# Two attentions over an image: group statistics by transfers, and Wk folded into the query projection

## The chip, the cores and the metric

The kernel runs on one core of one Trainium2 chip. The metric is device time in microseconds of one execution, taken as the median of several runs. A core has a matrix engine (TensorE, PE in the profile, with its weight loads shown as PEld), a vector engine (VectorE, DVE), an activation engine (ScalarE, ACT), GpSimd (POOL), an engine that here only starts transfers (SyncE, SP), and 16 DMA engines.

## The reference, cut to what matters

Two attention layers follow each other over x of shape (8, 64, 64, 64), that is 8 images of 64 channels and 4096 positions, all float32. Layer 0 has keys and queries of 8 channels and no scaling. Layer 1 normalises by groups of 8 channels first, has 64 channels of keys and queries, and a projection of its output.

```python
# layer 0 (n = 4096 positions, C8 = 8)
f = einsum('oc,bcn->bon', Wf, xf) + bf
g = einsum('oc,bcn->bon', Wg, xf) + bg
hh = einsum('oc,bcn->bon', Wh, xf) + bh
beta = softmax(einsum('bci,bcj->bij', f, g), axis=2)
x = x + einsum('bcj,bij->bci', hh, beta)

# layer 1
xg = x.reshape(b, 8, 8, h, w)              # 8 groups of 8 channels
mu = mean(xg, axis=(2, 3, 4)); var = mean((xg - mu) ** 2, axis=(2, 3, 4))
xn = (xg - mu) * rsqrt(var + 1e-5) * gamma + beta
q, k, v = split(einsum('oc,bchw->bohw', w_qkv, xn) + b_qkv, 3, axis=1)
attn = softmax(einsum('bqc,bkc->bqk', q, k) * 64 ** -0.5)
out = einsum('bqk,bkc->bqc', attn, v)
x = einsum('oc,bchw->bohw', w_proj, out) + b_proj + x
```

## The kernel before

Batch b is one image. The 4096 positions of an image lie in two halves of 2048: partitions 0 to 63 hold the channels of the first half and 64 to 127 those of the second. A half is four chunks of 512 columns. Each layer of each image is a stage of four chunks by 16 steps. In a step of layer 1, TensorE makes scores (8 products of 64x64 weights by 512 columns), ScalarE takes their exponential into a tile e, and TensorE weighs the values with the e of the step before; VectorE adds all e of a chunk into esum for the denominators. The stages come in the order layer 0 of image 0, layer 0 of image 1, layer 1 of image 0, layer 0 of image 2, layer 1 of image 1, and so on, and end with layer 1 of image 7. The scores of layer 0 come in groups of up to seven banks, fewer where another piece of work takes a pair of banks in that step.

PSUM has eight banks. Two accumulate, and six are three pairs which scores and everything else take in turn:

```python
    pairs = [banks[:, 2 * k + 1 : 2 * k + 3, :] for k in range(3)]
    ...
    def pair():
        nonlocal turn
        if lent is not None:
            return pairs[lent]
        turn += 1
        return pairs[turn % 3]
```

gavg is a constant that averages over the eight channels of a group and both halves, as a matrix product:

```python
    gavg = const.tile([P, 2, GROUPS, GS], F32, name="gavg")
    nc.gpsimd.memset(gavg, 0.5 / GS)
        ...  # affine_select keeps only the channels of the own group
```

What layer 1 of one image needs is prepared during an earlier stage, in units of (step, work, whether it takes a pair of banks). For image 0 that stage is layer 0 of image 1; for image b from 1 on it is layer 1 of image b - 1:

```python
        def before(self):
            ...
            def channels():
                vector.bn_aggr(mv, self.st())

            def means():

                ps = pair()
                matmul(ps[:, 0, 0:1], gavg, mv[:, 0:1], start=True, stop=True)
                nc.scalar.copy(mu, ps[:, 0, 0:1])
                d = small.tile([P, 1], F32, tag="d", name=f"d_{n}")
                vector.tensor_sub(d, mv[:, 0:1], mu)
                vector.scalar_tensor_tensor(v, d, d, mv[:, 1:2], op0=ALU.mult, op1=ALU.add)

            def deviations():
                ps = pair()
                matmul(ps[:, 0, 0:1], gavg, v, start=True, stop=True)
                ve = small.tile([P, 1], F32, tag="ve", name=f"ve_{n}")
                nc.scalar.copy(ve, ps[:, 0, 0:1])
                vector.tensor_scalar_add(ve, ve, EPS)
            ...  # four Newton steps for 1 / sqrt(ve), then times gamma, into self.a

            def normal(c):
                xns[c] = work.tile([P, CW], F32, tag="xn", bufs=1, name=f"xn_{n}_{c}")
                vector.tensor_scalar(
                    xns[c], x_tiles[self.b][:, ts(c, CW)], mu, self.a,
                    op0=ALU.subtract, op1=ALU.mult,
                )

            def begin():
                self.parts = self.own(F32)
                self.project(0, xns[0])

            at = [18, 22, 26] if self.b == 0 else [16, 20, 24]
            units = [(at[0], channels, False), (at[1], means, True), (at[2], deviations, True)]
            for c in range(NC):
                s = 31 + 8 * c if self.b == 0 else 30 + 8 * c
                units += [
                    (s - 4, lambda c=c: normal(c), False),
                    (s, begin if c == 0 else lambda c=c: self.project(c, xns[c]), True),
                    (s + 2, lambda c=c: self.values(xns[c], k1["wvp"], c), True),
                ]
            return units

        def project(self, c, xn):


            ps = pair()
            for i in range(2):
                for h in range(2):
                    matmul(
                        ps[ts(h ^ i, C), h, :], k1["wqk"][ts(h, C), i, :], xn[ts(h, C), :],
                        start=True, stop=True,
                    )
            cols = ts(c, CW)
            for h in range(2):
                nc.scalar.activation(
                    self.parts[:, h, cols], ps[:, h, :], AF.Identity,
                    bias=k1["qkb"][:, h : h + 1],
                )
                nc.sync.dma_start(
                    self.parts[ts(h, C), 2, cols], self.parts[ts(1 - h, C), h, cols]
                )

        def scores(self, ps, t, p, c):
            for m in range(2):
                for h in range(2):
                    matmul(
                        ps[ts(m, C), h, :],
                        self.parts[ts(h, C), 2 if p == h else 1 - h, ds(t * P + m * C, C)],
                        self.parts[ts(h, C), h, ts(c, CW)], start=True, stop=True,
                    )
```

`self.own` takes one of two buffers of a tile kq of (128, 3, 2048): part h holds q of half h in the partitions of that half and k of half h in the opposite ones, and part 2 takes k over into the partitions of its own half by a transfer, so that products of every half with every half find key and query in the same partitions. The weights Wv and Wproj are already multiplied into wvp before the start. The constants of layer 1 are made in three turns (`transposed`, `product`, `biases`) during the second chunk of layer 0 of image 0, each of which takes a pair of banks.

Of the kernel before, what the change touches and what calls it, by code (L numbers as in the profile page):

```python
# [9 lines left out]
F32 = mybir.dt.float32  # L10
# [58 lines left out]
def fast_path(  # L69
# [52 lines left out]
    made_last = {}  # L122
    tight = False
# [25 lines left out]
    def matmul(*args, **kwargs):  # L149
        in_order(nc.tensor.matmul(*args, **kwargs))  # L150

# [79 lines left out]
    gavg = const.tile([P, 2, GROUPS, GS], F32, name="gavg")  # L231
    nc.gpsimd.memset(gavg, 0.5 / GS)
    for h in range(2):
        for half in range(2):
            rows = gavg[ts(half, C), h, :, :]
            nc.gpsimd.affine_select(
                out=rows, in_=rows, compare_op=ALU.is_ge, fill=0.0,
                base=0, pattern=[[-GS, GROUPS], [0, GS]], channel_multiplier=1,
            )
            nc.gpsimd.affine_select(  # L240
                out=rows, in_=rows, compare_op=ALU.is_ge, fill=0.0,
                base=GS - 1, pattern=[[GS, GROUPS], [0, GS]], channel_multiplier=-1,
            )
    gavg = gavg.rearrange("p h g s -> p (h g s)")


    QP = 2 * CW // P
    stash = const.tile([P, (2 * B * NC - 1) * QP], F32, name="stash")
    recips = [dram.tile([P, QP], F32, name=f"recips_{i}") for i in range(2 * B * NC)]
# [3 lines left out]
    def layer1_constants():  # L253


        wqk = const.tile([P, 2, C], F32, name="wqk")
        for h in range(2):
            nc.gpsimd.dma_start(
                wqk[ts(h, C), :, :], WqkvT[:, 0 : 2 * C].rearrange("m (i c) -> m i c", i=2)
            )  # L260
        wp = twice("wp", WpT)
        wv = const.tile([C, C], F32, name="wv")
        nc.gpsimd.dma_start(wv, WqkvT[:, 2 * C : 3 * C])

        qkb = const.tile([P, 2], F32, name="qkb")
        for h in range(2):
            for i in range(2):
                nc.gpsimd.dma_start(
                    qkb[ts(h, C), i : i + 1], column(bqkv[ds(C if i != h else 0, C)])
                )  # L270
# [4 lines left out]
        wvt = const.tile([C, 2, C], F32, name="wvt")  # L275
        wvp = const.tile([P, C], F32, name="wvp")
        more = const.tile([P, 3], F32, name="more")
        k1.update(wqk=wqk, qkb=qkb, gam=gam, pb=pb, wvp=wvp)

        def transposed():  # L280
            t0 = pair()
            in_order(nc.tensor.transpose(t0[:C, 0, 0:C], wv, ident[0:C, 0:C]))
            for h in range(2):
                nc.scalar.copy(wvt[:, h, :], t0[:C, 0, 0:C])

        def product():
            t1 = pair()
            matmul(
                t1[:, 0, 0:C], wvt.rearrange("m h c -> m (h c)"), wp[0:C, :],
                start=True, stop=True,  # L290
            )
            nc.scalar.copy(wvp, t1[:, 0, 0:C])

        def biases():
            t2 = pair()
            for h in range(2):
                rows = ts(h, C)
                for i in range(2):
                    matmul(
                        t2[rows, h, i : i + 1], wqk[rows, i ^ h, :], bet[rows, :],  # L300
                        start=True, stop=True,
                    )
                matmul(t2[rows, h, 2:3], wvp[rows, :], bet[rows, :], start=True, stop=False)
                matmul(t2[rows, h, 2:3], wp[rows, :], vb[rows, :], start=False, stop=True)
            for h in range(2):
                nc.scalar.copy(more[ts(h, C), :], t2[ts(h, C), h, 0:3])
# [1012 lines left out]
```

## Time and profile before

| | |
|---|---|
| time, median of 3 runs | 3051.95 us (3050.56 to 3053.05) |
| span of the profiled execution | 3050.3 us |
| TensorE busy | 3023.2 us, 25857 matmul records |
| VectorE busy | 2596.0 us |
| ScalarE busy | 2036.3 us |
| L150 PE MATMUL banks<-xn_l,wqk (the projection of q and k) | 256 records, 35.5 us |
| L669 ACT ACTIVATE kq_l<-banks,qkb (its copies out of PSUM) | 64, 40.6 us |
| PE MATMUL banks<-mv_l,gavg and banks<-v_l,gavg (the statistics) | 16 records each, 3.0 and 3.1 us |
| DMA queues | 62.89 MB, mean 21 GB/s |

A group is named by source line, engine, operation, and what it writes and reads (output <- inputs, partitions x elements). All matrix products have line 150 and nearly all VectorE work line 140, since helpers record them, so groups are told apart by their tiles. A float32 product shows as two records, one per pass. Busy times overlap between engines; a share of busy time does not say which engine sets the end, for which there is the chain of work that ended last, followed back from the last instruction. The ends of matmuls are modelled, so their starts are the surer reading.

### The profile page before, as it was taken

How to read it: one execution, taken by the hardware profiler on the slowest of the kernel's cores; microseconds unless marked ns; L12 is line 12 of the kernel's file. 1: busy time of each engine (PE TensorE's matmuls, PEld its weight loads, DVE VectorE, ACT ScalarE, POOL GpSimd, SP SyncE). 2: the span in 40 equal slices, each digit the busy share in tenths (PEclk: the TensorE clock that was granted, in tenths of full speed). 3: DMA queues.
4: the chain of work that ended last, by engine and by line, in shares of the span. 5: the costliest groups of instructions: out<-in, count | busy, mean ns of one | idle time of the engine just before them, and what ended most of it. 6: DMA issues, size and time to landing. Idle time of an engine off the chain costs nothing.

```text
span 3050.3 us, 58859 instructions
## 1 busy us (share of the span) xinstructions
PE 3023.2 (99%) x25857; PEld 1287.4 (42%) x25857; DVE 2596.0 (85%) x1668; ACT 2036.3 (67%) x1972; POOL 16.7 (1%) x45
## 2 busy tenths in 40 slices
PE   8999999999999999999999999999999999999998
PEld 3333335433354333533345333453334533345555
DVE  6999987899778998789987899779997799877776
ACT  6878655786557865578655785558855588555554
POOL 2000000000000000000000000000000000000000
PEclk9999999999999999999999999999999999999999
DMA  3000010100101001010010100100001000000000
GB/s 79 22 8 11 19 40 16 32 1 15 40 19 29 1 15 40 22 25 1 16 40 23 25 1 15 43 22 22 1 22 40 19 8 1 16 22 16 9 15 13
DMA packets 69816, 62.89 MB, mean 21 GB/s; under 512 B 43104, under 2 KB 43152, under 8 KB 69552
## 3 DMA queue, kind: packets, MB, share of 16 engines
q1 hardware_dynamic: 68560, 58.90, 8.0%
q8 instruction: 204, 3.34, 0.5%
q14 instruction: 60, 0.49, 0.1%
q0 software_dynamic: 672, 0.12, 0.0%
q10 hardware_dynamic: 320, 0.04, 0.0%
HBM read 25.06 MB, written 8.65 MB: 11 GB/s over the span
## 4 chain that ended last, share of the span: by engine, by line
PE 95%; DVE 3%; issue 1%; ACT 1%; DMA 0%; SPq 0%; DVEq 0%; ACTq 0%
PE banks L150 95%; DVE esum_l L140 3%; ACT e_l L917 1%; DMA x<-in_x_dram 0%; ACT full_l L542 0%; DVE rt L140 0%; DVE w_l L140 0%; DVE x L140 0%; SPq L179 0%; DVE raw_l L140 0%; DVE st_l L140 0%; DVE raw_end L140 0%; DVE guess_l L140 0%; DVE xn_l L140 0%; DVEq L140 0%
## 5 line engine op out<-in xcount | busy, mean ns | idle before, releaser
L140 DVE TENSOR_TENSOR esum_l<-esum_l,e_l 128x2048 f32<-128x2048 f32 x895 | 2048.7, 2289 | 363.5 <-ACT e_l L876 313.5
L876 ACT ACTIVATE e_l<-banks 128x1024 f32<-128x1024 f32 x1024 | 992.7, 1021 | 782.8 <-PE banks L150 761.0
L150 PE MATMUL banks<-e_l,v_l 64*64 64x512 f32 (+2 forms) x8772 | 1118.2, 588 | 0.0
L917 ACT ACTIVATE e_l<-banks 128x512 f32<-128x512 f32 (+3 forms) x767 | 956.9, 1311 | 194.0 <-PE banks L150 178.1
L150 PE MATMUL banks<-kq_l 64*64 64x512 f32 (+1 forms) x8448 | 1028.3, 586 | 3.4 <-ACT e_l L917 3.2
L150 PE MATMUL banks<-e_l,vt_l 128*64 128x512 f32 (+1 forms) x4060 | 832.1, 550 | 0.0
L150 PEld LDWEIGHTS banks<-e_l,v_l 64*64 64x64 f32 (+1 forms) x8772 | 439.7, 134 | 505.0 <-issue 466.8
L150 PEld LDWEIGHTS banks<-kq_l 64*64 64x64 f32 (+1 forms) x8448 | 422.9, 135 | 503.8 <-issue 468.3
L150 PEld LDWEIGHTS banks<-e_l,vt_l 128*64 128x64 f32 x4060 | 267.1, 137 | 471.3 <-issue 451.2
L150 PE MATMUL banks<-fg_l 32*128 32x512 f32 x1792 | 210.8, 460 | 6.4 <-ACT e_l L917 4.1
L150 PEld LDWEIGHTS banks<-fg_l 32*128 32x128 f32 x1792 | 85.9, 183 | 189.9 <-ACT e_l L917 139.1
L140 DVE TENSOR_TENSOR esum_l<-e_l,e_l 128x2048 f32<-128x2048 f32 x64 | 146.4, 2287 | 7.1 <-ACT e_l L876 7.1
L140 DVE TENSOR_TENSOR esum_l<-esum_l 128x1024 f32<-128x1024 f32 x63 | 76.9, 1221 | 0.9
L140 DVE TRANSPOSE_TENSOR_REDUCE part_l<-esum_l 128x32 f32<-128x1024 f32 x32 | 63.1, 1973 | 0.0
L140 DVE COPY raw_l<-banks 128x512 f32<-128x512 f32 x31 | 21.4, 692 | 30.6 <-PE banks L150 30.6
L140 DVE TENSOR_TENSOR raw_l<-raw_l,r_l 128x512 f32<-128x512 f32 x63 | 43.2, 685 | 0.0
L669 ACT ACTIVATE kq_l<-banks,qkb 128x512 f32<-128x512 f32 x64 | 40.6, 696 | 0.0
L150 PE MATMUL banks<-xn_l,wqk 64*64 64x512 f32 x256 | 35.5, 592 | 0.0
L150 PEld LDWEIGHTS banks<-wh,x 64*64 64x64 f32 x1024 | 25.3, 139 | 13.3 <-issue 12.4
L150 PEld LDWEIGHTS banks<-wvp,xn_l 64*64 64x64 f32 x1024 | 24.0, 134 | 13.0 <-issue 13.0
L577 ACT COPY raw_l<-banks 128x512 f32<-128x512 f32 x32 | 19.1, 596 | 11.6 <-PE banks L150 11.4
L140 DVE SCALAR_TENSOR_TENSOR x<-raw_l,hb,x 128x512 f32<-128x512 f32 x32 | 24.1, 752 | 1.1
(111 smaller groups left out, 404.4 us busy)
## 6 DMA issues: line engine op xcount, KB each, us to landing
r_l<-recips SPq DMA_DIRECT2D x126, 128.0 KB, 2.9
fg_l<-high_l SPq DMA_DIRECT2D x216, 64.0 KB, 2.0
kq_l<-kq_l SPq DMA_DIRECT2D x64, 128.0 KB, 2.3
out_dram<-raw_l SPq DMA_DIRECT2D x62, 128.0 KB, 2.4
x<-in_x_dram SPq DMA_DIRECT2D x30, 256.0 KB, 4.9
kq_l<-high_l SPq DMA_DIRECT2D x32, 64.0 KB, 2.0
part_l<-part_l SPq DMA_DIRECT2D x128, 4.0 KB, 1.8
zt_l<-zs_l SPq DMA_DIRECT2D x124, 1.0 KB, 1.7
```

The source lines that it names most:

```text
L140: it = getattr(nc.vector, name)(*args, **kwargs)
L150: in_order(nc.tensor.matmul(*args, **kwargs))
L577: nc.scalar.copy(raw, acc[0])
L669: nc.scalar.activation(self.parts[:, h, cols], ps[:, h, :], AF.Identity, bias=k1["qkb"][:, h : h + 1],)
L876: nc.scalar.activation(e[:, p], both_ps[p], AF.Exp, scale=at.scale)
L917: nc.scalar.activation(e.rearrange("k p h n -> k (p h) n")[:, first_ : first_ + n_, :], banks[:, bank : bank + n_, :], AF.Exp, scale=at.scale,
```

## The change

Two things change in layer 1.

The first is the statistics. The averages over a group of channels no longer come from products with gavg. VectorE's mean and variance of each channel (mv) are stored to DRAM, and four transfers bring to each partition the 16 pairs of its group, over both halves; VectorE reduces them. This frees TensorE and ScalarE and the pairs of banks of that work.

The second is the keys. Scores are q . k = (Wq x + bq) . (Wk x + bk), and the term with bk is the same for all keys of a query, so the softmax drops it. What is left is (Wk' Wq x + Wk' bq) . x: one matrix, made once, projects the query, and the keys are the normalised x itself. So a chunk needs half as many product columns: four products of 256 columns in place of four of 512. The normalised x now has a place of its own in the tile kq for the whole stage, and its copy with halves swapped is made by the same number of transfers as before, as soon as it is normalised. The constants need one more turn (`bias_kq`).

The new work is issued behind the last addition into esum (`behind`), which fixes its place in VectorE's order. The diff, cut:

```diff
+    def behind(work_):
+        def made():
+            with tc.issue_after(added):
+                work_()
+        return made
...
-    gavg = const.tile([P, 2, GROUPS, GS], F32, name="gavg")
-    nc.gpsimd.memset(gavg, 0.5 / GS)
...
+    moments = [dram.tile([P, 2], F32, name=f"moments_{b}") for b in range(B)]
...
         def transposed():
-            t0 = pair()
-            in_order(nc.tensor.transpose(t0[:C, 0, 0:C], wv, ident[0:C, 0:C]))
+            ps = pair()
+            for i in range(3):
+                in_order(nc.tensor.transpose(ps[:C, 0, ts(i, C)], w3[:, i, :], ident[0:C, 0:C]))
             for h in range(2):
-                nc.scalar.copy(wvt[:, h, :], t0[:C, 0, 0:C])
+                nc.scalar.copy(
+                    wt[:, :, h, :], ps[:C, 0, 0 : 3 * C].rearrange("m (i c) -> m i c", i=3)
+                )
 
         def product():
-            t1 = pair()
-            matmul(
-                t1[:, 0, 0:C], wvt.rearrange("m h c -> m (h c)"), wp[0:C, :],
-                start=True, stop=True,
-            )
-            nc.scalar.copy(wvp, t1[:, 0, 0:C])
+            ps = pair()
+            for i, (left, right) in enumerate(((wt[:, 0], wt[:, 1, 0, :]), (wt[:, 2], wp[0:C, :]))):
+                matmul(
+                    ps[:, i, 0:C], left.rearrange("m h c -> m (h c)"), right,
+                    start=True, stop=True,
+                )
+            nc.scalar.copy(wkq_wvp, ps[:, :, 0:C])
 
         def biases():
-            t2 = pair()
+            ps = pair()
+            matmul(ps[:C, 0, 0:1], w3[:, 0, :], bet[0:C, :], start=True, stop=True)
             for h in range(2):
                 rows = ts(h, C)
-                for i in range(2):
-                    matmul(
-                        t2[rows, h, i : i + 1], wqk[rows, i ^ h, :], bet[rows, :],
-                        start=True, stop=True,
-                    )
-                matmul(t2[rows, h, 2:3], wvp[rows, :], bet[rows, :], start=True, stop=False)
-                matmul(t2[rows, h, 2:3], wp[rows, :], vb[rows, :], start=False, stop=True)
-            for h in range(2):
-                nc.scalar.copy(more[ts(h, C), :], t2[ts(h, C), h, 0:3])
-            nc.vector.tensor_add(qkb, more[:, 0:2], qkb)
-            nc.vector.tensor_add(pb, more[:, 2:3], pb)
-
-        return [transposed, product, biases]
+                matmul(ps[rows, 1, 0:1], wvp[rows, :], bet[rows, :], start=True, stop=False)
+                matmul(ps[rows, 1, 0:1], wp[rows, :], vb[rows, :], start=False, stop=True)
+            nc.scalar.activation(qb, ps[:C, 0, 0:1], AF.Identity, bias=qb)
+            nc.scalar.activation(pb, ps[:, 1, 0:1], AF.Identity, bias=pb)
+
+        def bias_kq():
+            ps = pair()
+            matmul(
+                ps[:, 0, 0:1], wt[:, 1].rearrange("m h c -> m (h c)"), qb, start=True, stop=True
+            )
+            nc.scalar.copy(kqb, ps[:, 0, 0:1])
+
+        return [transposed, product, biases, bias_kq]
 
 
...
+            group = small.tile([P, 2, GS, 2], F32, tag="group", bufs=1, name=f"group_{n}")
+            mean, var = (group[:, :, :, i].rearrange("p s k -> p (s k)") for i in range(2))
+            d = small.tile([P, 2 * GS], F32, tag="d", bufs=1, name=f"d_{n}")
             def channels():
                 vector.bn_aggr(mv, self.st())
+                sent = moments[self.b]
+                nc.sync.dma_start(sent, mv)
+                for s in range(2):
+                    rows = sent[ts(s, C), :].rearrange("(g k) i -> g (k i)", k=GS)
+                    for h in range(2):
+                        nc.sync.dma_start(
+                            group[ts(h, C), s, :, :],
+                            rows.unsqueeze(1).broadcast_to([GROUPS, GS, 2 * GS]),
+                        )
             def means():
-                ps = pair()
-                matmul(ps[:, 0, 0:1], gavg, mv[:, 0:1], start=True, stop=True)
-                nc.scalar.copy(mu, ps[:, 0, 0:1])
-                d = small.tile([P, 1], F32, tag="d", name=f"d_{n}")
-                vector.tensor_sub(d, mv[:, 0:1], mu)
-                vector.scalar_tensor_tensor(v, d, d, mv[:, 1:2], op0=ALU.mult, op1=ALU.add)
+                vector.tensor_reduce(mu, mean, axis=AX.X, op=ALU.add)
+                vector.tensor_scalar(mu, mu, 0.5 / GS, None, op0=ALU.mult)
+                vector.tensor_scalar(d, mean, mu, None, op0=ALU.subtract)
+                vector.tensor_mul(d, d, d)
+                vector.tensor_add(d, d, var)
+                vector.tensor_reduce(ve, d, axis=AX.X, op=ALU.add)
             def deviations():
-                ps = pair()
-                matmul(ps[:, 0, 0:1], gavg, v, start=True, stop=True)
-                ve = small.tile([P, 1], F32, tag="ve", name=f"ve_{n}")
-                nc.scalar.copy(ve, ps[:, 0, 0:1])
-                vector.tensor_scalar_add(ve, ve, EPS)
+                vector.tensor_scalar(ve, ve, 0.5 / GS, EPS, op0=ALU.mult, op1=ALU.add)
                 guess = small.tile([P, 1], I32, tag="guess", name=f"guess_{n}")
                 vector.tensor_single_scalar(
...
                 vector.tensor_mul(self.a, y, k1["gam"])
             def normal(c):
-                xns[c] = work.tile([P, CW], F32, tag="xn", bufs=1, name=f"xn_{n}_{c}")
+                if c == 0:
+                    parts = self.own(F32)
+                    self.q, self.x, self.swapped = (parts[:, i, :] for i in range(3))
+                cols = ts(c, CW)
                 vector.tensor_scalar(
-                    xns[c], x_tiles[self.b][:, ts(c, CW)], mu, self.a,
+                    self.x[:, cols], x_tiles[self.b][:, cols], mu, self.a,
                     op0=ALU.subtract, op1=ALU.mult,
                 )
-
-            def begin():
-                self.parts = self.own(F32)
-                self.project(0, xns[0])
-
-            at = [18, 22, 26] if self.b == 0 else [16, 20, 24]
-            units = [(at[0], channels, False), (at[1], means, True), (at[2], deviations, True)]
+                for h in range(2):
+                    nc.sync.dma_start(self.swapped[ts(h, C), cols], self.x[ts(1 - h, C), cols])
+            at = [18, 23, 26] if self.b == 0 else [16, 22, 24]
+            units = [
+                (at[0], channels, False),
+                (at[1], behind(means), False),
+                (at[2], behind(deviations), False),
+            ]
             for c in range(NC):
                 s = 31 + 8 * c if self.b == 0 else 30 + 8 * c
                 units += [
-                    (s - 4, lambda c=c: normal(c), False),
-                    (s, begin if c == 0 else lambda c=c: self.project(c, xns[c]), True),
-                    (s + 2, lambda c=c: self.values(xns[c], k1["wvp"], c), True),
+                    (s - 4, behind(lambda c=c: normal(c)), False),
+                    (s, lambda c=c: self.project(c), True),
+                    (s + 2, lambda c=c: self.values(self.x[:, ts(c, CW)], k1["wvp"], c), True),
                 ]
             return units
-        def project(self, c, xn):
+        def project(self, c):
             ps = pair()
+            width = CW // 2
+            cols = [ds(c * CW + i * width, width) for i in range(2)]
             for i in range(2):
                 for h in range(2):
                     matmul(
-                        ps[ts(h ^ i, C), h, :], k1["wqk"][ts(h, C), i, :], xn[ts(h, C), :],
-                        start=True, stop=True,
+                        ps[ts(h ^ i, C), i, 0:width], k1["wkq"][ts(h, C), :],
+                        self.x[ts(h, C), cols[i]], start=True, stop=True,
                     )
-            cols = ts(c, CW)
+            nc.scalar.activation(
+                self.q[:, cols[0]], ps[:, 0, 0:width], AF.Identity, bias=k1["kqb"]
+            )
             for h in range(2):
+                other = ts(1 - h, C)
                 nc.scalar.activation(
-                    self.parts[:, h, cols], ps[:, h, :], AF.Identity,
-                    bias=k1["qkb"][:, h : h + 1],
-                )
-                nc.sync.dma_start(
-                    self.parts[ts(h, C), 2, cols], self.parts[ts(1 - h, C), h, cols]
+                    self.q[ts(h, C), cols[1]], ps[other, 1, 0:width], AF.Identity,
+                    bias=k1["kqb"][other, :],
                 )
         def scores(self, ps, t, p, c):
             for m in range(2):
                 for h in range(2):
+                    keys = self.x if p == h else self.swapped
                     matmul(
-                        ps[ts(m, C), h, :],
-                        self.parts[ts(h, C), 2 if p == h else 1 - h, ds(t * P + m * C, C)],
-                        self.parts[ts(h, C), h, ts(c, CW)], start=True, stop=True,
+                        ps[ts(m, C), h, :], keys[ts(h, C), ds(t * P + m * C, C)],
+                        self.q[ts(h, C), ts(c, CW)], start=True, stop=True,
                     )
```

## The prediction

> **What bounds the kernel now.** I read the page first: busy shares, then the chain that ended last.
>
> ```profile
> PE 3023.2 (99%) x25857; PEld 1287.4 (42%) x25857; DVE 2596.0 (85%) x1668; ACT 2036.3 (67%) x1972; POOL 16.7 (1%) x45
> ...
> PE 95%; DVE 3%; issue 1%; ACT 1%; DMA 0%; SPq 0%; DVEq 0%; ACTq 0%
> ```
>
> TensorE (PE) is busy 99% of the 3050.3 us span and carries 95% of the chain. A busy PE need not be a PE at its peak, so I looked at how the chain lies in time (columns: start, length, what).
>
> ```profile
> 264.71 2.30 DVE esum_l L140
> 267.03 1.23 DVE esum_l L140
> 268.72 2.21 DVE esum_l L140
> 272.95 294.58 PE banks L150 x2778
> 570.39 107.73 PE banks L150 x606
> 678.14 265.03 PE banks L150 x2524
> 946.04 107.72 PE banks L150 x604
> 1053.77 265.03 PE banks L150 x2517
> ```
>
> There are two regimes. From about 145 to 273 us, where layer 0 of batches 0 and 1 runs with nothing of layer 1 beside it, the chain is mostly one 2.3 us VectorE addition into esum after another. From 272.95 us on it is PE, repeating with a period of 1053.77 - 678.14 = 375.63 us: one layer-1 stage and one layer-0 stage per batch. Seven of the eight layer-1 stages prepare the next batch's layer 1, and there the change acts. So I read TensorE in time inside the first of them (start, length, what).
>
> ```profile
> 404.96 1.90 PE L150 MATMUL banks<-e_l,v_l 64*64 64x512 f32 x16
> 406.68 1.90 PE L150 MATMUL banks<-kq_l 64*64 64x512 f32 x16
> 408.50 0.38 PE L150 MATMUL banks<-mv_l,gavg 128*128 128x1 f32 x2
> 408.81 1.95 PE L150 MATMUL banks<-e_l,v_l 64*64 64x512 f32 x16
> 410.58 1.90 PE L150 MATMUL banks<-kq_l 64*64 64x512 f32 x16
> ...
> 420.88 1.90 PE L150 MATMUL banks<-kq_l 64*64 64x512 f32 x16
> 422.71 0.38 PE L150 MATMUL banks<-v_l,gavg 128*128 128x1 f32 x2
> 423.02 1.95 PE L150 MATMUL banks<-e_l,v_l 64*64 64x512 f32 x16
> 424.79 1.90 PE L150 MATMUL banks<-kq_l 64*64 64x512 f32 x16
> ...
> 442.81 1.90 PE L150 MATMUL banks<-kq_l 64*64 64x512 f32 x16
> 444.53 1.04 PE L150 MATMUL banks<-xn_l,wqk 64*64 64x512 f32 x8
> 445.39 1.90 PE L150 MATMUL banks<-e_l,v_l 64*64 64x512 f32 x16
> 447.11 1.47 PE L150 MATMUL banks<-kq_l 64*64 64x512 f32 x12
> ```
>
> Read the starts, not the lengths (ends are modelled and overlap). Scores to weighing, or weighing to scores, is always 1.715 us: 16 records, which are 8 products in two passes, four at a time in the four 64x64 quarters, so four rounds of 0.429 us. A whole step is 3.43 us (410.58 to 414.01, and so on). What stands between scores and weighing comes wholly on top: nothing hides it.
>
> **What the Trainium skill says.** "TensorEngine Tiling (Array Packing)", section Key Properties: tiles work independently, and changing the tiling mode drains the engine. The trace agrees: a 128x1 product with gavg moves one column, yet the step around it, 406.68 to 410.58, is 3.90 us instead of 3.43, 0.47 us more, and the weighing after it starts slowly too (1.77 us instead of 1.715). "TensorE: Matmul & The Clock Gate", section Back-to-back issue gap: a product's spacing is N/2.4 ns plus 2.5 for N columns at the full clock, with a floor of about 60 cycles. For 512 columns that is 0.216 us. The trace has 0.429 us per round, twice as much, so here one pass costs two cycles per column; of the page I keep only that the spacing goes with the columns. A round of 256 columns is then estimated at 0.215 us. "ScalarE: Activation LUTs", section What ACT_TABLE_LOAD costs: an ACTIVATE with a bias pointer takes about 280 + 0.833 N ns. For N = 512 that is 706; the page has 696 for kq_l<-banks,qkb. For 256 it gives an estimate of 0.49 us. "DMA: Bandwidth & Descriptors", section Two DMAs through the same engine are not ordered: a transfer that reads what another wrote must wait for the first one's completion. So the statistics take two latencies in a row; for small transfers the page shows 1.4 us (recips) and 1.7 (zt).
>
> **The change part by part.**
>
> *Projection.* Before: four products of 512 columns per chunk, one round in each of two passes. Step 442.81 to 447.11 is 4.30 us, so 0.865 over 3.43. After: four of 256 in the same four quarters, 2 x 0.215 = 0.43. Saved 0.43 per chunk, four chunks per stage: 1.73 us.
>
> *Statistics.* Two products with gavg leave the PE: 3.90 - 3.43 = 0.47, and 424.79 - 420.88 - 3.43 = 0.48, so 0.95 us per stage. In their place: one store of mv, four loads of group, and on VectorE two reductions (about 0.20 each, as zt_l<-part_l) and four small operations (about 0.155) for one of 0.15 and one of 0.22: 1.02 - 0.37 = 0.65 us more per batch. VectorE is busy 179.8 of the 227 us from 345 to 572, so this lies beside the PE. Wait for the loads: store 1.4, four issues of about 0.6 (the part_l transfers need 2.56 us for four), landing 2 or 3, so about 7 us; aggregation at step 16 and use at step 22 are six steps apart, 20.6 us. Hidden. The sixteen fg transfers behind them in the queue start some 5 us later and are not needed until the stage ends, over 100 us on.
>
> *Keys.* The normalised x is written into the kq tile and swapped by the same 64 transfers of 128 KB (2.3 us), only four steps earlier; needed a stage later. Hidden. There are two buffers of kq, and the one taken was last read a whole stage earlier, so taking it four steps sooner waits for nothing.
>
> *ScalarE.* Two evictions of 696 ns become one of 128x256 and two of 64x256, about 0.49 each: 1.47 against 1.39 us. After a projection ScalarE idles 1.20 us before the next exponential, so it fits, and the pair of banks is needed only one step later.
>
> *Once only.* Constants get two more transposes, one more product and a fourth turn that takes a pair of banks in layer 0 of batch 0; there a smaller group of scores costs one more change of tiling, about 0.4 us. Estimated +0.5 us, at about 110 us where the chain is still PE.
>
> *Layer 0 of batch 1* (145 to 337 us) prepares the first layer 1. The PE loses four projections (1.7 us) and two gavg products that each took a pair; VectorE gains 0.65 us, and loses the 0.62 us that it waited for ve_l. VectorE is the chain until 273 us; after it the PE is, but VectorE is at 96%. I count -0.8 us.
>
> Sum: seven stages x (1.73 + 0.95) = 18.8; +0.5 - 0.8; in all -19.1 us: 3051.95 - 19.1 = 3032.9, rounded to 3033.
>
> **Rivals.**
> First, a round of 256 columns isn't half as long, because four weight loads or a fixed cost bound it. Against: the value products (64 columns, 32 records, eight rounds) stretch a step by 450.54 to 454.44 less 3.43 = 0.47 us, 0.059 per round, so the loads keep up far below 0.215. If it were so all the same, only 7 x 0.95 would be left: 3045.
> Second, VectorE or a late transfer becomes the wait. VectorE runs its additions in order, so a late group would hold every following addition, then the e tiles, then ScalarE and PE. For: at 145 to 273 us it is already the chain, and there only five steps of about 2.3 us, 11.5 us, lie between aggregation and use. Against: 7 us suffices. If the first batch misses by a few us: 3036 to 3038; if all batches did (not believed, 13 us of slack): up to 3055.
> Third, ScalarE's three smaller evictions hold back the next exponentials. It would show as PE waits of about 0.1 to 0.3 us in 28 steps, at most 8 us: 3041. Against it the 1.20 us of idle time.
> Fourth, the smaller groups and their rearrangement in layer 0 of the first two batches (28 more products of 256 columns stand in place of 14 of 512) cost 2 or 3 us: 3036.
>
> **Range and chances.** The seven stages are regular to 0.01 us and carry nearly all; what is loose is the stretch before 340 us, give or take 2 us, the repeats, which spread over 2.5 us, and a small part for the rivals, all on the slow side. So 3029 to 3038. 2% is 61 us; the groups of PE that the change shortens or removes are busy for 35.5 us (xn_l by wqk) and 6.1 us (both with gavg) in all, so faster by over 2% is as good as excluded, and slower needs a wait of 10 us per stage, which nothing shows.
>
> **What would show it.** The period 678 to 1053 should fall from 375.63 to 372.95 us. The step with a projection should take 3.86 us, and no step at the statistics over 3.43. The group kq_l by wkq_wvp should hold 256 records of 256 columns. DVE should not idle ahead of the first reduction of group. If the projection step takes 4.3 the first rival holds; if mu_l waits for a transfer, the second; if PE waits for the evictions of kq_l, the third. A layer-0 stage of other than 107.7 us on the chain would mean that something moved that I didn't see.

## The result, and the profile after

| | before | after |
|---|---|---|
| time, median of 4 runs each | 3052.5 us (3050.56 to 3053.83) | 3035.34 us (3034.77 to 3036.53) |
| ratio, after to before | | 0.9945, 95% interval 0.9928 to 0.9962 |
| span of the profiled execution | 3050.3 us | 3033.1 us |

So the changed kernel is 17.2 us shorter (0.55%), where 19.1 us was predicted: 3035.3 against 3033, inside the range of 3029 to 3038, and within 2%.

The busy shares and the shares of the chain that ended last, after:

```profile
PE 3003.4 (99%) x25853; PEld 1320.3 (44%) x25853; DVE 2597.6 (86%) x1698; ACT 2040.7 (67%) x1988; POOL 10.6 (0%) x31
...
PE 93%; DVE 4%; issue 1%; ACT 1%; DMA 0%; SPq 0%; DVEq 0%; ACTq 0%
```

TensorE is still the bound. Its busy time fell by 19.8 us, and its share of the chain by two points. The chain in time, after (start, length, what), shows the period:

```profile
568.77 107.71 PE banks L151 x596
676.49 262.39 PE banks L151 x2515
941.75 107.71 PE banks L151 x595
1049.47 262.37 PE banks L151 x2506
...
2541.77 479.48 PE banks L151 x4454
```

1049.47 - 676.49 = 372.98 us, where 375.63 was the period before. The pieces of 107.71 us (107.73 before) are the first part of a layer-0 stage, not the whole of it: the stage goes on until the first weighing of the next layer 1, at 716.31 us (717.95 before), 39.82 us behind 676.49 (before: 39.81 us behind 678.14). So nothing came out of the layer-0 stage, and all of it out of the layer-1 stage. TensorE in time, in the first layer-1 stage after (start, length, what), shows where:

```profile
411.13 1.90 PE L151 MATMUL banks<-kq_l 64*64 64x512 f32 x16
412.85 1.90 PE L151 MATMUL banks<-e_l,v_l 64*64 64x512 f32 x16
414.56 1.90 PE L151 MATMUL banks<-kq_l 64*64 64x512 f32 x16
...
442.89 1.90 PE L151 MATMUL banks<-kq_l 64*64 64x512 f32 x16
444.61 0.61 PE L151 MATMUL banks<-kq_l,wkq_wvp 64*64 64x256 f32 x8
445.04 1.90 PE L151 MATMUL banks<-e_l,v_l 64*64 64x512 f32 x16
446.75 1.90 PE L151 MATMUL banks<-kq_l 64*64 64x512 f32 x16
```

Where the products with gavg stood, scores now follow each other in 414.56 - 411.13 = 3.43 us. The step with a projection takes 446.75 - 442.89 = 3.86 us, and its weighing starts 0.43 us later than it would without one (445.04 - 444.61). The groups of the changed work (form, count, busy us, mean ns of one, idle before):

```profile
L151 PE MATMUL banks<-kq_l,wkq_wvp 64*64 64x256 f32 x256 | 21.8, 379 | 0.0
L685 ACT ACTIVATE kq_l<-banks,kqb 64x256 f32<-64x256 f32 x64 | 30.1, 470 | 1.2
L680 ACT ACTIVATE kq_l<-banks,kqb 128x256 f32<-128x256 f32 x32 | 15.3, 478 | 0.0
```

The projection is 21.8 us where it was 35.5. Its copies are 45.4 us where they were 40.6, and the idle column of L685 holds 1.2 us that did not exist before.

Divided at the same points, the two chains account for the whole difference (us):

| stretch | before | after | difference | predicted |
|---|---|---|---|---|
| start to the first weighing of layer 1 of image 0 | 342.30 | 343.32 | +1.02 | +0.5 - 0.8 = -0.3 |
| from there to the same product inside layer 0 of image 2 (678.14, 676.49) | 335.84 | 333.17 | -2.67 | -2.68 |
| five periods (to 2556.33, 2541.77) | 1878.19 | 1865.28 | -12.91 | -13.40 |
| the rest, with the seventh such stage | 493.97 | 491.33 | -2.64 | -2.68 |
| sum | 3050.3 | 3033.1 | -17.20 | -19.1 |

Two places miss. In the five periods, one (1422.44 to 1795.80) is 0.39 us longer than its neighbours. And in the first 343 us, which should have gained a little, the change loses. The runs below first split the gain, and then look for that loss.

In that early stretch the starts of two runs differ by up to 1.8 us, so I count from one mark: the start of VectorE's last addition of the first chunk of layer 0 of image 0 (68.44 us before, 67.69 after). From there to the first weighing it is 273.86 us before and 275.63 after: a loss of 1.77 us.

### The profile page after: what moved, and what is told of

It is laid out like the page before. It is cut to its first block, busy times and chain, and to the rows that moved or that the text cites. A ratio compares the mean times of both kernels' runs of the same rounds, so it can differ in the third digit from the quotient of the medians.

```text
span 3033.1 us, 58936 instructions
## 1 busy us (share of the span) xinstructions
PE 3003.4 (99%) x25853; PEld 1320.3 (44%) x25853; DVE 2597.6 (86%) x1698; ACT 2040.7 (67%) x1988; POOL 10.6 (0%) x31
## 4 chain that ended last, share of the span: by engine, by line
PE 93%; DVE 4%; issue 1%; ACT 1%; DMA 0%; SPq 0%; DVEq 0%; ACTq 0%
PE banks L151 93%; DVE esum_l L141 3%; ACT e_l L923 1%; DMA x<-in_x_dram 0%; ACT full_l L539 0%; DVE x L141 0%; DVE st_l L141 0%; DVE raw_l L141 0%; DVE high_l L141 0%; ACT kq_l L685 0%; DVE rt L141 0%; DVE w_l L141 0%; SPq L189 0%; DVE raw_end L141 0%; DVE guess_l L141 0%
## 5 line engine op out<-in xcount | busy, mean ns | idle before, releaser
L151 PE MATMUL banks<-e_l,v_l 64*64 64x512 f32 (+1 forms) x8792 | 1122.3, 586 | 0.0
L923 ACT ACTIVATE e_l<-banks 128x1536 f32<-128x1536 f32 (+3 forms) x766 | 956.8, 1312 | 195.9 <-PE banks L151 180.1
L151 PEld LDWEIGHTS banks<-e_l,v_l 64*64 64x64 f32 (+1 forms) x8792 | 459.3, 133 | 484.8 <-issue 427.7
L151 PEld LDWEIGHTS banks<-kq_l 64*64 64x64 f32 (+1 forms) x8448 | 440.6, 135 | 488.5 <-issue 443.5
L685 ACT ACTIVATE kq_l<-banks,kqb 64x256 f32<-64x256 f32 x64 | 30.1, 470 | 1.2
L151 PEld LDWEIGHTS banks<-wkq_wvp,kq_l 64*64 64x64 f32 x1024 | 24.8, 134 | 12.6 <-issue 11.9
L151 PE MATMUL banks<-wh,x 64*64 64x64 f32 x1024 | 24.2, 223 | 0.3 <-ACT full_l L539 0.3
```

The costliest lines, as they stand in the source:

```text
L685: nc.scalar.activation(self.q[ts(h, C), cols[1]], ps[other, 1, 0:width], AF.Identity, bias=k1["kqb"][other, :],)
L923: nc.scalar.activation(e.rearrange("k p h n -> k (p h) n")[:, first_ : first_ + n_, :], banks[:, bank : bank + n_, :], AF.Exp, scale=at.scale,
```

## The experiments

Each kernel ran beside the kernel before on the same chip. The kernel before had medians of 3050.89, 3051.14 and 3050.35 us there, for the first, second and third group of runs.

### One part at a time

The statistics by transfers alone; projection, keys and constants as before. Against the changed kernel:

```diff
-        matmul(ps[ts(h ^ i, C), i, 0:width], k1["wkq"][...], self.x[ts(h, C), cols[i]], ...)
+        matmul(ps[ts(h ^ i, C), h, :], k1["wqk"][ts(h, C), i, :], xn[ts(h, C), :], ...)
```

> The kernel before with the statistics by transfers alone; q and k are still projected by four products of 512 columns. Theory A (the gain is TensorE time inside the layer-1 stages, 0.93 us per stage for the two products with gavg and the changes of tiling around them; layer 0 of the first two images is paced by VectorE and gains nothing): the period from one layer-1 stage to the next is 375.64 - 0.93 = 374.7 us, the time 3052.5 - 6.5 = 3046.0, give or take 1.5. Rival B (the gain is the TensorE busy time taken out, wherever it is: 6.1 us for gavg): 3046.4, but with a seventh of it ahead of 340 us. Rival C (the statistics give nothing, all comes from the keys): 3052.

The keys alone; the statistics with gavg as before:

```diff
-                vector.tensor_reduce(mu, mean, axis=AX.X, op=ALU.add)
-                ...
+                ps = pair()
+                matmul(ps[:, 0, 0:1], gavg, mv[:, 0:1], start=True, stop=True)
+                nc.scalar.copy(mu, ps[:, 0, 0:1])
```

> The changed kernel with the statistics put back on TensorE (gavg, each taking a pair of banks). Theory A: the period falls by 4 x 0.43 = 1.72 us to 373.9, the time to 3052.5 - 12.0 + 1.0 = 3041.5, give or take 1.5, if the lost microsecond ahead of 345 us belongs to the keys and their evictions; 3040.5 if it belongs to the new place of the statistics. Rival B: 13.7 us of TensorE busy time less, 3038.8.

Measured: 3045.77 us for the statistics (ratio 0.9983, 0.9976 to 0.999) and 3039.76 us for the keys (0.9961, 0.9947 to 0.9975). The chain of the statistics alone, the two pieces that hold a layer-1 stage each:

```profile
676.52 264.09 PE banks L151 x2515
...
1051.20 264.08 PE banks L151 x2521
```

and of the keys alone:

```profile
675.68 263.33 PE banks L151 x2523
...
1049.62 263.33 PE banks L151 x2526
```

The periods, each the mean of five, are 374.67 and 373.93 us where before has 375.64: the statistics are worth 0.97 per stage and the keys 1.71, against 0.95 and 1.73 predicted. They add up to 2.68, where the changed kernel has 2.66, so neither hides the other. Against the kernel before on that chip the totals fell by 5.1 and 11.1 us, where seven stages give 6.8 and 12.0. From the mark to the first weighing the profiles have 274.51 us for the statistics and 274.48 for the keys, 0.65 and 0.62 more than before: each part gives a little back in the early stretch.

### The cost of a round of 256 columns

Every image but the first does its projection twice over, into the same place, so the work is repeated and nothing else moves:

```diff
-            for i in range(2):
+            for i in [0, 1] if self.b == 0 else [0, 1, 0, 1]:
                 for h in range(2):
                     matmul(ps[ts(h ^ i, C), i, 0:width], ...)
```

> The changed kernel with the four products of 256 columns made twice over in every chunk of images 1 to 7; the second four write the same numbers again. Theory A (nothing hides a projection, and a round of 256 columns is 0.215 us): 28 chunks x 0.43 = 12.0 us more than the changed kernel, 3047.4, and a step with a projection takes 4.29 us instead of 3.86. Rival (TensorE has slack around the projection, or a round of 256 is bound by weight loads): 3035 to 3041, or 3059 if a round of 256 took the time of one of 512.

Measured: 3046.78 us (0.9985, 0.9979 to 0.9992). TensorE in time, the same step:

```profile
443.14 1.90 PE L151 MATMUL banks<-kq_l 64*64 64x512 f32 x16
444.86 1.04 PE L151 MATMUL banks<-kq_l,wkq_wvp 64*64 64x256 f32 x16
445.72 1.90 PE L151 MATMUL banks<-e_l,v_l 64*64 64x512 f32 x16
447.44 1.90 PE L151 MATMUL banks<-kq_l 64*64 64x512 f32 x16
```

The step is 447.44 - 443.14 = 4.30 us, 0.44 more than with one projection, and the span is 12.3 us longer, where 7 x 4 x 0.43 = 12.0 was expected. Sixteen records of 256 columns cost what eight of 512 did. The first rival, that the round is bound by something other than its columns, is refuted.

### How much slack the transfers of the statistics have

The statistics are used one step after they are stored instead of five or six:

```diff
-            at = [18, 23, 26] if self.b == 0 else [16, 22, 24]
+            at = [18, 19, 26] if self.b == 0 else [16, 17, 24]
```

> The changed kernel with the averages used one step after the aggregation instead of five or six, so that the two transfers in a row, about 7 us, lie open before VectorE. Theory A (VectorE has slack in the layer-1 stages and five e tiles in hand; it paces layer 0 of image 1): in the layer-1 stages VectorE waits some 3.5 us and the period stays at 373.0 us; in layer 0 of image 1 it waits about 4.5 us and all of it shows: 3035.3 + 4 = 3039, give or take 1. Rival (VectorE's order passes every wait on to the exponentials and to TensorE): seven stages x 3 us more, 3060.

Measured: 3037.19 us (0.9952, 0.9935 to 0.9968), 1.85 us more than the changed kernel. The chain in time at the first image's statistics has the transfers on it now,

```profile
222.78 2.88 DMA moments<-mv_l
...
227.72 1.98 DMA group_l<-moments
```

and of VectorE's waits for the group there is one in the whole run (total us, times, longest us):

```profile
DVE mu_l L141 <- DMA group_l<-moments: 3.6, 1, 3.6
```

From the end of the aggregation (222.76) to the landing of the last group (229.70) it is 6.9 us: the 7 us of the prediction. With one step of distance VectorE loses 3.6 us where it sets the pace (layer 0 of image 1) and nothing in the layer-1 stages, whose period stays 372.97. I had expected waits there too, hidden ones; none is recorded. With the distance of the changed kernel there is no such wait at all, and the second rival is refuted.

### The copies of q in layer 0 of image 1

In the early stretch, the chain of the changed kernel (start, length, what) has something that the kernel before does not show:

```profile
249.87 1.46 ACT e_l L923
251.38 20.18 PE banks L151 x130
271.59 1.72 issue
273.32 0.59 ACT e_l L923
273.91 0.36 ACT kq_l L680
274.30 0.47 ACT kq_l L685
274.78 0.48 ACT kq_l L685
275.31 37.20 PE banks L151 x280
```

Twice (here and at 312.5) it leaves TensorE and runs through ScalarE: an exponential, then the three copies of a projection, which empty the pair of banks that the next scores take. To test it, image 0 gets two copies in place of three. This leaves out the exchange of halves of its q for the second 256 columns, so that its scores there take the other half's queries; the other images are untouched.

```diff
+            if self.b == 0:
+                nc.scalar.activation(
+                    self.q[:, cols[1]], ps[:, 1, 0:width], AF.Identity, bias=k1["kqb"]
+                )
+                return
             for h in range(2):
                 other = ts(1 - h, C)
```

> The changed kernel, but for image 0 alone q of the second 256 columns of a chunk is copied out of PSUM by one 128-partition ACTIVATE in place of two of 64 partitions; this leaves out the exchange of halves, so image 0's q is not the reference's. Theory A2 (ahead of 345 us TensorE, faster by 0.43 us per projection, only waits at the next group of scores until ScalarE has cleared the pair of banks; ScalarE has 0.47 us less to do here): the waits of TensorE for kq at about 275 and 316 us go, layer 1 of image 0 begins 1 us earlier, and the time is 1 us under the changed kernel's. Rival A1 (VectorE alone paces that stretch): no change in when layer 1 of image 0 begins, same time within 0.3 us.

Measured: 3032.6 us (0.9941, 0.9925 to 0.9958), 2.7 us less than the changed kernel. The same stretch of its chain:

```profile
248.83 1.46 ACT e_l L928
250.29 0.04 issue
250.33 95.95 PE banks L151 x693
```

TensorE is unbroken. From where it takes over to the first weighing it is 340.97 - 250.33 = 90.64 us, against 343.32 - 251.38 = 91.94. So the third copy costs 1.30 us here. TensorE's starts show where: of the same products, those of the changed kernel start 1.05 us later at the take-over, 1.66 us later behind the first of the two places (276.53 against 274.87) and 2.33 us later behind the second (317.27 against 314.94). The spans differ by 2.4 us (3033.1 and 3030.7); the other 1.04 is that run's earlier start (the mark at 66.65 against 67.69), which I can't lay to the copies. The third rival is true in this one stage, and only there: in the layer-1 stages after, no copy of kq stands on the chain.

Two attempts at the same gain with nothing left out. The two copies of halves go to VectorE for image 0 (`vector.tensor_scalar_add` in place of the two `nc.scalar.activation`):

> The changed kernel, but for image 0 the two 64-partition copies of q out of PSUM are VectorE's instead of ScalarE's; nothing is left out. Theory A2 (the pair of banks is held up by ScalarE's queue): the waits of TensorE for kq at about 275 and 316 us go if VectorE comes to it in time, and up to 1.3 us with them. Rival A1 (VectorE paces): two more operations of about 0.35 us per chunk, 2.8 us more in VectorE's chunks, and as much more time.

And the projection of image 0 is issued ahead of the group of scores of its step, not behind it, so that its copies start earlier:

> The changed kernel, but for image 0 each projection is issued ahead of its step's group of scores and its copies ahead of that step's exponentials. Theory A2: ScalarE clears the pair of banks before TensorE comes to the next group, so TensorE waits for no kq; the exponentials start up to 1.4 us later, and if those lie on the loop of e tiles this eats the 1.3 us. Expected 0 to 1.3 us under the changed kernel. Rival A1: no change.

Measured: 3037.41 us (0.9955, 0.9941 to 0.9969) and 3034.63 us (0.9949, 0.9935 to 0.9963). With the copies on VectorE its sixth to eighth chunk grow by 0.89, 1.87 and 0.87 us and TensorE now waits 2.4 us for VectorE's kq: worse. With the early projections TensorE no longer waits for kq, but its waits for the exponentials in 140 to 350 us grow from 6.0 to 7.6 us, and from the mark to the first weighing it is 275.99, no better. The chain still goes through the copies. From 250 to 340 us of the changed kernel ScalarE is busy for 73.3 of 90 us; its exponentials alone take 68.4 us (17 of 2048 columns at 1.875 us, 12 of 1536 at 1.451, 10 and 2 of 1024 at 1.02, 12 of 512 at 0.597). That its time is what is short here, and not the order of its work, fits this but is not shown. (Splitting the score products so that the halves need not be exchanged wasn't tried.)

### The constants

The fourth turn is folded into the third, by accumulating Wk' (Wq beta + bq) in one product group:

```diff
-            matmul(ps[:C, 0, 0:1], w3[:, 0, :], bet[0:C, :], start=True, stop=True)
             for h in range(2):
                 rows = ts(h, C)
+                matmul(ps[rows, 0, 0:1], wkq[0:C, :], bet[0:C, :], start=True, stop=False)
+                matmul(ps[rows, 0, 0:1], wt[:, 1, h, :], qb, start=False, stop=True)
...
-        return [transposed, product, biases, bias_kq]
+        return [transposed, product, biases]
```

> The changed kernel with the bias of the folded query made in the turn of the other biases, from beta and bq directly, so that the constants take three turns of a pair of banks and not four. Theory A3 (the fourth turn costs 0.7 us of VectorE's second chunk, 41.19 against 40.46 us): that chunk falls back to 40.5 us and the time is 0.7 us under the changed kernel's, unless the shifted groups of scores give it back. Rival (the turn is hidden beside VectorE and the 0.7 us is the projection or a transfer): 41.2 us, same time.

and once more together with the copies on VectorE:

> Both, the biases in three turns and image 0's q copied by VectorE in part. If both gains stand and add up, 1 to 2 us under the changed kernel; if the grouping of scores gives back what the turn saves, as in the run with three turns, the same as the run with VectorE's copies.

Measured: 3033.86 us (0.9945, 0.9928 to 0.9961) and 3035.8 us (0.9951, 0.9937 to 0.9964). The second chunk of VectorE's additions, in which the constants are made, takes 40.46 us before, 41.19 after, 40.50 with three turns. So the fourth turn costs 0.69 us of that chunk, and all the new constants 0.73, not the 0.4 of a change of tiling that I counted within the 0.5. The runs with three turns lie 1.5 us below those of the changed kernel repeated below (3033.27 to 3034.79 against 3035.02 to 3036.23), but in another group of runs, and the intervals of the ratios overlap. From the mark to the product inside layer 0 of image 2 it is 608.64 us (67.22 to 675.86), against 608.80 in the first profile of the changed kernel and 610.17 in the second; the second, like this one, has 6.8 us at half clock in the early stretch and the first 3.4 (see below), so 1.53 is the fairer difference. With the copies on VectorE in both, the three turns are 1.6 us faster within one group of runs (3035.8 against 3037.41), and those ranges overlap too. Both point the same way; whether it is the better version is not settled.

### Relief for VectorE

If VectorE set the pace to the end of layer 0 of image 1, giving its work away would bring the whole part back. GpSimd normalises image 0 (`eng = nc.gpsimd if self.b == 0 else vector`):

> The changed kernel with the four normalisations of image 0 (128x512, 0.54 us each on VectorE) on GpSimd, which is idle there. Theory A1 (VectorE paces layer 0 of the first two images): the four chunks of image 1 come sooner by 0.5 us each, and the time is 1.5 to 2 us under the changed kernel's, 3033. Rival A2 (ScalarE and the pair of banks pace it): under 0.5 us.

and makes the Newton steps of image 0 too:

> As the run before, and the four Newton steps of image 0 on GpSimd too, which takes another 2.3 us from VectorE. Theory A1: VectorE's chunk around 250 us falls from 41.2 to about 38.5 us, and the time is 3 to 4 us under the changed kernel's, as far as TensorE's idle time there (about 5 us) allows. Rival A2: under 0.5 us. Rival (GpSimd is slower than the steps allow and holds back the projections): more time than the changed kernel.

Measured: 3035.21 us (0.9949, 0.9932 to 0.9965) and 3051.96 us (1.0004, 0.9995 to 1.0013). In the first, the four normalisations run on GpSimd from 245.41 to 257.79 us, 3.10 us each. VectorE's sixth chunk, beside them, is longer by 1.28 us, and its seventh and eighth are shorter by 0.73 and 0.46. Yet from TensorE's take-over (251.88) to the first weighing (343.81) it is 91.93 us, as in the changed kernel (91.94): neither moves it. So from 251 us on VectorE does not set the pace; TensorE does, 22 us sooner than before (272.95).

In the second, TensorE waits once for GpSimd's normal (total us, times, longest), and GpSimd in time shows why:

```profile
PE banks L151 <- POOL kq_l L652: 19.7, 1, 19.7
```

```profile
260.65 2.32 POOL L638 TENSOR_TENSOR w_l<-guess_l 128x1 f32<-128x1 f32 x1
263.05 1.18 POOL L639 TENSOR_TENSOR w_l<-w_l,ve_l 128x1 f32<-128x1 f32 x1
264.31 0.19 POOL L642 TENSOR_SCALAR w_l<-w_l 128x1 f32<-128x1 f32 x1
...
264.85 0.19 POOL L638 TENSOR_TENSOR w_l<-guess_l 128x1 f32<-128x1 f32 x1
```

One operation on 128 numbers takes 2.3 us for as long as VectorE adds, and the same operation 0.19 us once VectorE's last addition has ended (264.17). The Trainium skill, "SBUF — State Buffer", section Who interferes with whom, says that a VectorE instruction with two inputs in SBUF contends with a GpSimd instruction that reads SBUF, and its section Summary: rules for kernel authors adds that the one that comes second is blocked until the first has finished. The trace agrees: 2.3 us is one addition of e into esum, 2.29 us.

### The same kernel again

> The changed kernel once more, as the measure for the runs beside it on the same chip. Theory A: period 372.98 us; first weighing of layer 1 of image 0 some 275.6 us after the end of VectorE's first chunk, at 343 us; 3034 to 3035.

Measured: 3035.40 us (0.995, 0.9937 to 0.9964), as the first time. The kernel before, though, has 3050.35 us beside it, so the gain is 15.0 us here, not 17.2. The 4 runs of the kernel before in the first comparison had a median of 3052.5 us, the 62 in the experiments have medians of 3050.35 to 3051.14: some 2 us of the 17.2 belong to those 4 runs, and the gain is 15 to 17 us.

From the mark to the first weighing it is 277.00 us, 1.37 more than in the first profile of the same kernel, and the chain shows in which piece:

```profile
250.62 21.56 PE banks L151 x128
```

21.56 us where the first profile has 20.18. In both, the same work. What differs is TensorE's granted clock. In these traces it changes at steps of 3.41 us; the windows between such steps (us, busy of PE, PEld, DVE, ACT, POOL, granted TensorE clock, DMA share, GB/s) are, in the first profile,

```profile
249.26:252.67 3.41, 1.80 (x16) 0.78 (x17) 3.31 (x4) 2.17 (x4) 0.00 (x0) 1.00 0.33 75
252.67:256.08 3.41, 3.41 (x12) 0.96 (x8) 3.31 (x2) 3.04 (x4) 0.00 (x0) 0.50 0.03 7
```

in the second

```profile
246.99:250.40 3.41, 1.65 (x12) 0.48 (x8) 3.41 (x3) 2.89 (x2) 0.00 (x0) 1.00 0.00 0
250.40:253.81 3.41, 3.19 (x15) 1.35 (x17) 3.31 (x2) 2.69 (x4) 0.00 (x0) 0.50 0.34 77
253.81:257.23 3.42, 3.42 (x12) 0.84 (x9) 3.21 (x3) 1.15 (x3) 0.00 (x0) 0.50 0.02 5
```

in the kernel before

```profile
225.04:228.46 3.42, 1.40 (x11) 0.95 (x13) 3.39 (x4) 2.46 (x3) 0.00 (x0) 1.00 0.00 0
228.46:231.87 3.41, 3.41 (x14) 0.61 (x10) 3.31 (x2) 1.07 (x2) 0.00 (x0) 0.50 0.00 0
```

and with the keys alone

```profile
247.22:250.64 3.42, 3.22 (x19) 1.25 (x19) 3.38 (x2) 2.52 (x3) 0.00 (x0) 1.00 0.34 77
```

Read the clock, the sixth number after the length, and TensorE's busy time, the first. The first profile has a spell of 3.41 us at half clock, which loses TensorE 1.7 us; in the second it lasts 6.83 us and loses 3.4, and of the second's 1.7 more the chain shows 1.37. The kernel before has a spell too, at 228 us, but there VectorE sets the pace and is busy for 3.31 of 3.41 us: it costs nothing. In both profiles of the changed kernel it lies behind 250.4 us, on TensorE's chain. The keys alone have no spell in the early stretch.

The Trainium skill, "TensorE: Matmul & The Clock Gate", section What's actually happening, says that the clock is halved after an idle window of about 3.4 us and full again after a busy one, and that the window runs freely, so that its effect differs between runs of one kernel. The halves, the steps of 3.41 us and the difference between runs agree. That the window must be idle does not: between 40 us and the last 20 us of all fourteen profiles, the window ahead of each of the thirteen spells has TensorE busy for up to 57% of it (53% and 48% above), and no window at full clock with 59.8% or more is followed by one. A spell lasts until a window in which TensorE is busy throughout; windows with 85 to 95% (here 3.19 of 3.41 us) did not end it. (The ends of matmuls are modelled, so these shares are not exact.)

## Why the prediction was right, and where it was not

**The bound and the stages: right.** Both regimes, the period (372.95 predicted, 372.98 measured), the step of 3.86 us, the 3.43 us at the statistics, 0.95 and 1.73 us for the two parts (0.97 and 1.71 alone), 256 records of 256 columns. Seven stages should give 18.76 us; they gave 18.22. Of the 0.54 us that is missing, 0.39 is in the one longer period. The same period is longer in six and normal in five of the eleven profiles of kernels with both parts; its cause is open. Two readings were off and cost nothing: 107.7 us is not a whole layer-0 stage (that takes 147.56 us on the chain, from 570.39 to 717.95 before), and layer 0 of image 1 begins on TensorE at 172.77 us, not 145.

**The estimates: right.** Copies of 256 columns 0.478 us, against 0.49; store and loads 6.9 us, against 7; VectorE's six operations are 0.174 + 0.154 + 0.235 + 0.174 + 0.174 + 0.170 = 1.08 us, which is 0.71 more than what they replace, against 0.65. The keys' transfers, four steps earlier, are waited for nowhere.

**Rivals one and two: refuted,** as the prediction had it. The fourth, the regrouping in layer 0, came about in the numbers foreseen (1144 records of 256 columns where 1088 were, 3524 of 512 where 3552 were); what it costs I did not measure by itself.

**The step that failed** is "Layer 0 of batch 1 ... I count -0.8 us", and the third rival that I put aside by the 1.20 us of idle time of ScalarE. That idle time was read in a layer-1 stage; in layer 0 of image 1 ScalarE is busy for 73.3 of 90 us, with exponentials of up to 1.875 us in place of 1.02. From the mark to the first weighing the loss is 1.77 us where a gain of 0.3 stood:

- the constants: +0.73 us measured in VectorE's second chunk, +0.5 predicted. Mis-sized.
- the third copy: +1.30 us, shown by the run with two copies; nothing was counted for it.
- the half clock: up to +1.7 us, in a place where before it was free. That such a spell delays the chain is shown by the two runs of the same kernel, where 3.4 us more of it cost 1.37 us. That it comes here is the change's doing: just ahead TensorE waits 0.52 and 1.46 us for exponentials (at 249 and 251 us), and in ten of the eleven profiles of kernels with both parts some stretch of 3.41 us between 240 and 265 us has TensorE busy for 42% or less (in the eleventh, with the late statistics, the long wait and the spell come at 228 to 239 us), while before and with either part alone none there is under 88%. Why TensorE waits for the exponentials there only with both parts is open.
- what remains, 1.77 - 0.73 - 1.30 - 1.7 = -2.0 us, is a remainder, not a measurement: fewer products and fewer waits of VectorE would be gains, but that the pieces add up is not shown. The keys alone have the same constants and three copies, on the chain as well, and no spell, and lose only 0.62 us.

So what the prediction lacked is that as TensorE's work shrinks and the end of VectorE's rule comes earlier (at 251 in place of 273 us), the waits of TensorE in that stretch, and its half clock, become the chain's. That the gain of 17.2 us comes so near to the predicted 19.1 is in part luck: against the other runs of the kernel before it is some 2 us smaller.

No variant beats the changed kernel beyond doubt. The run with two copies is the fastest, but leaves work out; the three turns of constants are the one to try further.

## What to carry to other kernels

Where one engine's instructions follow each other without a gap over hundreds of microseconds, the cost of taking some away can be read from the starts of their neighbours, to 0.02 us per stage. In the stretches between regimes it can't: ask there which engine will set the pace after the change and what it waits for, and read the slack of the others in that very stretch. Before comparing two profiles to a microsecond, compare two profiles of the same kernel.

## What was not expected of the hardware

In twelve of fourteen profiles TensorE lost 1.7 or 3.4 us of clock between 144 and 348 us, in one spell of 3.4 or 6.8 us at half speed; one profile has none, and in one, where TensorE waits 19.7 us, the spell lasts 20.5 us. Each follows a window of 3.41 us in which TensorE was busy for 57% or less. The spells begin where it is not the bound, and last a little beyond that: if it becomes the bound meanwhile, they cost up to 1.7 us for each 3.4 us. Two runs of one kernel differed by 3.4 us of it.

GpSimd's operations on 128 numbers took 2.3 us, not 0.19, beside VectorE's 2.29 us additions of two tiles. A block of 128x512 normalised on GpSimd took 3.10 us there, against 0.54 on VectorE.
